# Moving the norm steps of the first batch to the wide tables in a two-layer graph attention kernel

## The chip, the cores and the metric

The kernel runs on one core of a Trainium2 chip. The metric is the device time of one execution in microseconds (us); lower is better. The core has a matrix engine (PE, with its weight loads shown apart as PEld), a vector engine (DVE), a scalar engine (ACT), GpSimd (POOL) and a queue that only issues transfers (SP). Each works through its own instructions in the order in which the program puts them there.

## The reference, cut to what matters

```
x = layernorm(x + L0(x, adj))          # x: (8, 2048, 256) f32, adj: (2048, 2048) int32
x = layernorm(x + L1(x, adj))

L0: q, k, v = x @ W.T + b              # 4 heads of 64
    s = clip(q k / 8, -10, 10); s = -10 where adj == 0
    softmax of s within each of 8 chunks of 256 keys; ctx = sum over chunks of attn @ v
    out = layernorm(ctx @ Wo.T + bo + x) * gamma + beta
L1: Wh = h @ W; e = leaky_relu(s_src + s_dst); softmax over the neighbours; elu(alpha @ Wh)
```

The result of the first line is called x1 below. Layer 1 needs x1 times W and times the two attention vectors (264 columns in all), with x1 turned so that its 256 features lie along the partitions.

## The kernel before, in words

The batches are taken one after the other. The attention of layer 0 of one batch is cut into 64 slots. Slot s stands for a query group q of 512 rows (q = s // 16, four groups), one of two head pairs and one of 8 key chunks; i = s % 16 is the place of the slot in its query group. In batch b the slots of layer 0 carry, interleaved, the layer 1 work of batch b-1 (lower.step, L799). Batch 0 has no layer 1 beside it. There the slots carry the mask steps instead (masks.step, L210), until they run out.

The order on every engine is written out by hand in the slot loop, L922 to L990. One slot does this, in this order:

- SP: the stores of the mask step before (send, L194), the mask piece of slot s+3 (load_slab, L361), and further loads named below.
- DVE: the reciprocal rd of slot s-1 (L427), then clip and mask of the scores of slot s+1, two instructions of 128x1024 that write pr (L388). They need the scores ps on PE (L377) and the slab.
- DVE: the norm steps that a table puts "beside" (L966).
- PE: product(s, 0) (L412), which needs the exponentials of slot s; then ACT: the copy raw (L419) and the two exponentials of slot s+1 (L400).
- The mask step (L976), where batch 0 still has one: SP loads a piece of adj (L216), PE turns the piece before it (L238), DVE writes clip (L240), ACT writes edge (L242), DVE writes ab (L228). The stores of clip and edge (L248, L251) go out at the head of the next slot, on SP. The tiles clip and edge have two buffers each, so that the clip of slot s waits until the clip of slot s-2 has been stored.
- PE: product(s, 1), ACT: its copy raw.
- The steps that tables put "behind" (L981 to L988): first those of the group before the current one (after), then the sending of a finished context, then those of the current group (behind).

From q = 1 on, an object Between (L501) carries query group q-1 through the rest of layer 0, between the slots of query group q. Its steps, with their instructions:

- Between(...) itself loads x into xg (512 KB, SP, L262).
- bias and shift: one DVE addition of 128x1024 each (L512, L516).
- output: 4 matmuls for two blocks of 128 rows (L527), into psM.
- add: DVE, from psM, two blocks (L538). stats: DVE, two blocks (L477, L480); the second call also makes rs and off (L485 to L488, DVE and POOL).
- a.apply: four ACT instructions (L492). scale, again: one DVE instruction each (L544, L547).
- finish: four ACT instructions, then ACT issues the store of x1 to x1D (L552).
- load: eight SP transfers of 64 KB that read x1D back in squares of 32x32 (L271, through load_squares). turn: one DVE transpose within squares (L283), which makes x1T.
- values of one block: matmuls of x1T with w1 (L571) into psM, and two ACT copies (L578, L582).

The context of a head pair goes out through ctxD (ACT) and comes back over SP (load_context, L447), and turn_context (L452, one DVE transpose of 128x512) writes it into qT. It stands at i = 3, and at i = 8+3 = 11, or at i = 8+6 = 14 where the flag wide is set (L961).

Which table is used is decided at i = 0 of each query group:

```
wide = b > 0 and 0 < q < NCH - 1
...
if not b:
    beside, behind, after = BESIDE_0, BEHIND_0, AFTER_0
```

So batch 0 uses the compact tables, with load at i = 12, turn and the first values at i = 15, and the other three values in the first three slots of the next query group. Batches 1 to 7 use the wide tables for q = 1 and 2. After slot 63 a list of pieces (order, L1022) finishes the batch; in batch 0 it begins with values 1, 2 and 3 of group 2.

Of the kernel before, what the change touches and what calls it, by code (L numbers as in the profile page):

```python
# [22 lines left out]
def adj_resnorm_kernel(  # L23
# [23 lines left out]
    NCH = N // CH  # L47
# [146 lines left out]
    def send():  # L194
        while outgoing:
            outgoing.pop(0)()
# [201 lines left out]
    def exps(s, u):  # L398
        pr = probs[s][u]
        nc.scalar.activation(pr, pr, AF.Exp, scale=0.125)  # L400
# [100 lines left out]
    class Between:  # L501
# [83 lines left out]

    AHEAD = {12: lambda o: o.load()}
    BESIDE = {  # L590
        1: [lambda o: o.bias()],
        4: [lambda o: o.add((0, 1))],
        5: [lambda o: o.add((2, 3)), lambda o: o.a.stats((0, 1))],
        6: [lambda o: o.a.stats((2, 3)), lambda o: o.shift()],
        8: [lambda o: o.scale()],
        9: [lambda o: o.again(), lambda o: o.b2.stats((0, 1))],
        10: [lambda o: o.b2.stats((2, 3))],
        14: [lambda o: o.turn()],
    }
    BEHIND = {  # L600
        3: lambda o: o.output((0, 1)),
        4: lambda o: o.output((2, 3)),
        7: lambda o: o.a.apply(o.y),
        11: lambda o: o.finish(),
        14: lambda o: o.values((0,)),
        15: lambda o: o.values((1,)),
    }

    WIDE_BESIDE = {
        1: [lambda o: o.bias()],  # L610
        4: [lambda o: o.add((0, 1))],
        5: [lambda o: o.add((2, 3))],
        6: [lambda o: o.a.stats((0, 1))],
        7: [lambda o: o.a.stats((2, 3))],
        8: [lambda o: o.shift()],
        10: [lambda o: o.scale()],
        11: [lambda o: o.again()],
# [3 lines left out]
    WIDE_BEHIND = {  # L621
        3: lambda o: o.output((0, 1)),
        4: lambda o: o.output((2, 3)),
        8: lambda o: o.a.apply(o.y),
        14: lambda o: o.finish(),
    }
    LATER_AHEAD = {0: lambda o: o.load()}
    LATER_BESIDE = {2: lambda o: o.turn()}
    LATER_BEHIND = {i: lambda o, i=i: o.values((i - 5,)) for i in range(5, 9)}

    BESIDE_0 = {i: steps for i, steps in BESIDE.items() if i != 14} | {15: BESIDE[14]}
    BEHIND_0 = {i: step for i, step in BEHIND.items() if i != 14} | {15: BEHIND[14]}
    AFTER_0 = {i: lambda o, i=i: o.values((i + 1,)) for i in range(3)}
    AFTER = {0: lambda o: o.values((2,)), 1: lambda o: o.values((3,))}

    def factors(b, sd, waug):

# [268 lines left out]
    for b in range(B):  # L906
        waug = blocks.tile([P, NT, H, D1], F32, tag="waug", name="waug")
        sd = small.tile([P, 2 * H, NT], F32, tag="sd", name="sd", bufs=1)
        if b == 0:
            for s in range(3):  # L910
                load_slab(s)
            scores(0)
            for u in range(KT):
                exps(0, u)
        if lower:
            for _ in range(STEP):
                lower.make()
        closing = Closing(b - 2, CLOSING) if b > 1 else None
        if closing:
            closing.do(-1)  # L920
        group = None
        for s in range(SLOTS):  # L922
            q, hp, c = where[s]
            i = s % QS
            send()
            if s + 3 < SLOTS:
                load_slab(s + 3)
            if i == 0:
                before = group
                group = Between(b, q - 1, sd, waug) if q else None  # L930
                wide = b > 0 and 0 < q < NCH - 1
                ahead = {} if wide else AHEAD
                later_beside = {}
                if not b:
                    beside, behind, after = BESIDE_0, BEHIND_0, AFTER_0
                else:
                    beside, behind = (WIDE_BESIDE, WIDE_BEHIND) if wide else (BESIDE, BEHIND)
                    after = {}
                    if q > 1:
                        later_beside, after = LATER_BESIDE, LATER_BEHIND  # L940
            if before and later_beside and i in LATER_AHEAD:
                LATER_AHEAD[i](before)
            if i == 1 and q:
                load_context(b, q - 1, 1)
            if i == QS // 2 + 1:
                load_context(b, q, 0)
            if group and i in ahead:
                ahead[i](group)
            if s == SLOTS - 3 and b + 1 < B:
                turns = [project(b + 1, g) for g in range(NCH)]  # L950
                turns[0].pop(0)()
            if s:
                normalize(s - 1)
            if s + 1 < SLOTS:
                scores(s + 1)

            if s == SLOTS - 1 and b + 1 < B:
                turns[0].pop(0)()
            if i == 3 and q:
                turn_context(q - 1, 1)  # L960
            if i == QS // 2 + (6 if wide else 3):  # L961
                turn_context(q, 0)
            if before and i in later_beside:
                later_beside[i](before)
            if group:
                for step in beside.get(i, ()):  # L966
                    step(group)
            elif closing:
                closing.do(s, behind=False)
            product(s, 0, not lower)  # L970
            if s + 1 < SLOTS:
                for u in range(KT):
                    exps(s + 1, u)
            if lower:
                if b + 1 < B or s < SLOTS - LATE:
                    lower.step()  # L976
            elif masks.left():
                masks.step()
            product(s, 1, not lower)

            if before and i in after:  # L981
                after[i](before)
            if i == 0 and q:
                send_context(b, q - 1, 1)
            if i == QS // 2:
                send_context(b, q, 0)
            if group and i in behind:
                behind[i](group)  # L988
            elif closing and not q:
                closing.do(s, beside=False)  # L990
        normalize(SLOTS - 1)

        send()
        before = group
        gd, fs = factors(b, sd, waug)
        group = None
        every = tuple(range(QT))

        def begin():
            nonlocal group  # L1000
            group = Between(b, NCH - 1, sd, waug)

        def ctx():
            context(NCH - 1, 1)

        steps = [
            lambda: group.bias(),
            lambda: group.output(every),
            lambda: group.add(every),
            lambda: (group.shift(), group.a.stats(every)),  # L1010
            lambda: group.a.apply(group.y),
            lambda: (group.scale(), group.again(), group.b2.stats(every)),
            lambda: group.finish(),
            lambda: group.turn_all(),
            lambda: group.values((0, 1)),
            lambda: group.values((2, 3)),
        ]
        if b + 1 < B:
            (k0, v0, q0), (l1, t1, k1, v1, q1), (l2, t2, k2, v2, q2), (l3, t3, k3, v3, q3) = turns
            rest = [lambda: lower.rest(1)] if lower else []  # L1020
            first = [] if b else [lambda: before.values((1,))]
            order = [begin, *rest, l1, *rest, *first, lambda: before.values((2, 3))]  # L1022
            order += [*rest, ctx, *rest, k0]
            order += [steps[0], t1, steps[1], v0, steps[2], steps[3], l2, k1, steps[4], q0]
            order += [steps[5], v1, t2, l3, steps[6], q1, steps[7], k2, steps[8], steps[9], t3, v2]
            order += [lambda: [load_slab(s) for s in range(3)], fs[0], q2, fs[1], k3, fs[2], v3]
            order += [lambda: scores(0), q3, lambda: [exps(0, u) for u in range(KT)]]
        else:

            step = lower.step  # L1030
            order = [begin, lambda: before.values((2, 3)), steps[0], step, ctx, step, steps[1], step]
            order += [steps[2], step, steps[3], step, steps[4], step, steps[5], step, steps[6], step]
            order += [steps[7], step, steps[8], step, steps[9], step, fs[0], step, fs[1], step, fs[2]]
            order += [step, lambda: lower.rest(4)]
            assert sum(p is step for p in order) == LATE
        for piece in order:
            send()
            piece()
        send()
        lower = Layer1(b, gd, waug)  # L1040
# [56 lines left out]
```

## Time and profile before

| | |
|---|---|
| median of 4 runs | 3794.96 us (3793.72 to 3796.33) |
| the profiled execution's own time | 3796.46 us |
| its span in the profile | 3794.7 us |
| mean granted PE clock | 0.992 |
| PE busy | 3680.2 us (97%) |
| DVE busy | 3196.1 us (84%) |
| ACT busy | 1946.9 us (51%) |
| POOL busy | 1388.1 us (37%) |
| slots of batch 0 with i = 0, by the reciprocal of the slot | slot 16 at 140.23, slot 32 at 229.89, slot 48 at 309.08 |
| last reciprocal of the slot loop of batch 0 (slot 63) | 381.29 us |
| first layer 1 instruction (L734) | 447.9 us |

In timelines, a line gives the start in us from the start of the span, the duration in us, the engine, the line of the kernel, the operation, the tile written and the tile read, the count, and in brackets how long the engine had been idle before and what ended that. A small q behind an engine's name is its queue of transfers. In tables by stretch, each engine has its busy time and its count of instructions; then come the granted PE clock (1.00 is full), the share of time in which the DMA engines were busy, and GB/s. In lists of waits, the three numbers are the total in us, how often, and the longest.

### The profile page before, as it was taken

To read this page: it belongs to the slowest core of one execution; us is meant where nothing else is said; L and a number is where in the kernel's file an instruction comes from. 1 tells how busy PE (TensorE), PEld (TensorE's weight loads), DVE (VectorE), ACT (ScalarE), POOL (GpSimd) and SP (SyncE) were. 2 spreads that over 40 slices of the span, in tenths; PEclk is the share of its full clock that TensorE was granted. 3 is DMA by queue.
4 is the path that set the end of the run, shared out by engine and by line. 5 is a ranking of instruction groups with operands and counts; after the bars stand their busy time and mean duration, and the time that the engine had idled before them with its cause. 6 is when DMAs were issued, how large, how long until landed. Compare 5 with 4: busy or idle time off the path is not lost. (4 is left out here: it accounts for less than half of the span.)

```text
span 3794.7 us, 160217 instructions
## 1 busy us (share of the span) xinstructions
PE 3680.2 (97%) x72100; PEld 2747.4 (72%) x72100; DVE 3196.1 (84%) x4810; ACT 1946.9 (51%) x3601; POOL 1388.1 (37%) x1202
## 2 busy tenths in 40 slices
PE   9999999999999999999999999999999999999787
PEld 5656677776777777776777767777677777776676
DVE  5876499986999789995999959998699968998798
ACT  4666345555555555554555545554555555555221
POOL 1445234433343343433444324433344434434310
PEclk9999999999999999999999999999999999999899
DMA  6652333333343433433434434433333334333354
GB/s 162 150 115 65 79 102 101 97 88 113 106 105 96 94 115 102 103 97 88 134 88 104 102 98 127 105 100 82 113 107 104 101 88 121 98 103 81 97 151 120
DMA packets 756545, 398.50 MB, mean 105 GB/s; under 512 B 425744, under 2 KB 721040, under 8 KB 755856
## 3 DMA queue, kind: packets, MB, share of 16 engines
q1 hardware_dynamic: 705856, 354.54, 36.1%
q10 hardware_dynamic: 50000, 33.70, 2.8%
q8 instruction: 564, 9.24, 1.0%
q14 instruction: 125, 1.02, 0.1%
HBM read 331.22 MB, written 56.89 MB: 102 GB/s over the span
## 5 line engine op out<-in xcount | busy, mean ns | idle before, releaser
L388 DVE SCALAR_TENSOR_TENSOR pr<-ps,slab 128x1024 f32<-128x1024 f32 x1024 | 1191.5, 1204 | 198.9 <-PE ps L377 194.2
L734 DVE SCALAR_TENSOR_TENSOR e<-srow,gd,et 128x640 f32<-128x640 f32 (+1 forms) x1536 | 1344.6, 931 | 11.4 <-PE pa L754 6.2
L412 PEld LDWEIGHTS pc<-vaug,pr 128*64 128x64 f32 x32768 | 1039.7, 138 | 411.6 <-issue 302.8
L412 PE MATMUL pc<-vaug,pr 128*64 128x65 f32 x32768 | 1156.4, 224 | 18.0 <-ACT raw L419 10.5
L754 PE MATMUL pa<-waug,e 128*64 128x65 f32 x32768 | 1081.0, 224 | 39.4 <-DVE e L734 38.0
L400 ACT ACTIVATE pr<-pr 128x1024 f32<-128x1024 f32 x1024 | 1045.3, 1056 | 74.3 <-DVE pr L388 63.1
L754 PEld LDWEIGHTS pa<-waug,e 128*64 128x64 f32 x32768 | 1020.2, 139 | 64.6 <-DVE e L734 37.7
L377 PE MATMUL ps<-qT,kT 64*128 64x512 f32 x4096 | 1025.4, 617 | 3.3 <-DVE pr L388 2.4
L419 ACT COPY raw<-pc 128x260 f32<-128x260 f32 x1024 | 384.7, 376 | 1232.8 <-PE pc L412 1206.5
L434 POOL TENSOR_TENSOR part<-raw,rd 128x512 f32<-128x512 f32 x448 | 467.9, 1044 | 1426.5 <-DVE rd L427 1412.1
L436 POOL TENSOR_TENSOR acc<-acc,part 128x512 f32<-128x512 f32 x448 | 574.9, 1283 | 35.2
L377 PEld LDWEIGHTS ps<-qT,kT 64*128 64x128 f32 x4096 | 349.8, 186 | 328.5 <-issue 223.3
L427 DVE RECIPROCAL rd<-raw 128x8 f32<-128x8 f32 x512 | 100.6, 197 | 102.7 <-ACT raw L419 101.0
L434 POOL TENSOR_TENSOR acc<-raw,rd 128x512 f32<-128x512 f32 x64 | 66.8, 1043 | 318.6 <-DVE rd L427 317.8
L782 ACT ACTIVATE hh<-pa,dn 128x64 f32<-128x64 f32 x512 | 114.8, 321 | 101.0 <-DVE dn L778 101.0
L571 PE MATMUL pw<-w_sb,x1T 128*128 128x264 f32 x512 | 140.6, 411 | 9.9 <-DVE x1T L283 9.4
L487 POOL TENSOR_TENSOR rs_c<-rs_c,nhalf 128x4 f32<-128x4 f32 x32 | 55.6, 1737 | 229.4 <-DVE off_c L486 229.4
L321 PE MATMUL pp<-xT,wk_sb 128*128 128x512 f32 x256 | 119.8, 612 | 7.9 <-ACT qT L329 6.6
L527 PE MATMUL po<-wo_sb,qT 128*128 128x256 f32 x512 | 125.0, 389 | 1.1 <-DVE qT L454 0.8
L321 PE MATMUL pp<-xT,wq_sb 128*128 128x512 f32 x256 | 116.2, 596 | 0.0
L337 PE MATMUL pv<-wv_sb,xT 128*128 128x256 f32 x512 | 115.9, 379 | 0.0
L571 PEld LDWEIGHTS pw<-w_sb,x1T 128*128 128x128 f32 x512 | 92.6, 194 | 31.5 <-DVE x1T L283 10.0
(93 smaller groups left out, 1858.1 us busy)
## 6 DMA issues: line engine op xcount, KB each, us to landing
et<-edgeD SPq DMA_DIRECT2D x256, 320.0 KB, 3.1
slab<-clipD SPq DMA_DIRECT2D x512, 128.0 KB, 3.3
et<-edgeD SPq DMA_DIRECT2D x128, 384.0 KB, 3.4
srow<-rowD SPq DMA_DIRECT2D x64, 320.0 KB, 4.3
xg<-in_x_dram SPq DMA_DIRECT2D x32, 512.0 KB, 5.4
x1D<-y ACTq DMA_DIRECT2D x32, 512.0 KB, 4.2
x1g<-x1D SPq DMA_DIRECT2D x32, 512.0 KB, 5.5
out_dram<-o SPq DMA_DIRECT2D x32, 512.0 KB, 3.9
```

The source lines that it names most:

```text
L321: nc.tensor.matmul(pps[c], lhsT=w[:, kc, c * P : (c + 1) * P], rhs=st["xT"][:, kc, :], start=(kc == 0), stop=(kc == KC - 1),)
L377: nc.tensor.matmul(ps[:, k, :], lhsT=kT[rows, hp, t * P : (t + 1) * P], rhs=qT[rows, hp, cols], start=True, stop=True,)
L388: nc.vector.scalar_tensor_tensor(pr, pss[u], -CLIP, slab[:, u, :].unsqueeze(1).to_broadcast([P, 2, CH]), op0=ALU.max, op1=ALU.min,)
L400: nc.scalar.activation(pr, pr, AF.Exp, scale=0.125)
L412: nc.tensor.matmul(pc[z * D : (z + 1) * D, i, :], lhsT=probs[s][u][:, k, i * P + z * D : i * P + (z + 1) * D], rhs=vaug[:, KT * c + u, 2 * ...
L419: nc.scalar.copy(raws[s][:, k], pc)
L434: nc.gpsimd.tensor_mul(part, raw[:, :, :, :D], rd.to_broadcast([P, 2, QT, D]))
L436: nc.gpsimd.tensor_add(accv, accv, part)
L527: nc.tensor.matmul(po[:, k, :], lhsT=qT[:, c, t * P : (t + 1) * P], rhs=wo_sb[:, c, :], start=(c == 0), stop=(c == KC - 1),)
L571: nc.tensor.matmul(pw[:, k, : F + 2 * H], lhsT=self.x1T[:, c, u * P : (u + 1) * P], rhs=w1_sb[:, c, :], start=(c == 0), stop=(c == KC - 1),)
L734: nc.vector.scalar_tensor_tensor(e[:, :w], self.rows[n][:, :w], self.gd[:, h, j : j + 1], self.edge[k // JG][:, j % JG, :w], op0=ALU.max, ...
L754: nc.tensor.matmul(self.pa[z * D : (z + 1) * D, i * D1 : (i + 1) * D1], lhsT=e[:, i * P + z * D : i * P + (z + 1) * D], rhs=self.waug[:, j ...
```

## The change

The flag wide no longer depends on the batch, and the special tables AFTER_0 and AFTER are gone. In batch 0, groups 0 and 1 (in q = 1 and q = 2) now take the wide tables, and their load, turn and values move into the next query group by the LATER tables, as in the other batches. Group 2 (in q = 3) keeps BESIDE_0 and BEHIND_0. The other batches and the pieces after slot 63 are as before. The program has the same number of rows on PE and on SP in both versions.

| step | i before (batch 0, groups 0 and 1) | i after |
|---|---|---|
| load of x | 0 | 0 |
| bias | 1 | 1 |
| output, two halves (behind) | 3, 4 | 3, 4 |
| add, two halves | 4, 5 | 4, 5 |
| stats of the first norm | 5, 6 | 6, 7 |
| shift | 6 | 8 |
| apply (behind) | 7 | 8 |
| scale | 8 | 10 |
| again | 9 | 11 |
| stats of the second norm | 9, 10 | 12, 13 |
| finish (behind) | 11 | 14 |
| turn_context of the first head pair | 11 | 14 |
| load of x1 in squares (head of the slot) | 12 | 0 of the next q, after the load of x |
| turn | 15 | 2 of the next q |
| values of four blocks (behind) | 15, and 0, 1, 2 of the next q | 5, 6, 7, 8 of the next q |

```
-    AFTER_0 = {i: lambda o, i=i: o.values((i + 1,)) for i in range(3)}
-    AFTER = {0: lambda o: o.values((2,)), 1: lambda o: o.values((3,))}
...
-                wide = b > 0 and 0 < q < NCH - 1
+                wide = 0 < q < NCH - 1
                 ahead = {} if wide else AHEAD
-                later_beside = {}
-                if not b:
-                    beside, behind, after = BESIDE_0, BEHIND_0, AFTER_0
+                if wide:
+                    beside, behind = WIDE_BESIDE, WIDE_BEHIND
                 else:
-                    beside, behind = (WIDE_BESIDE, WIDE_BEHIND) if wide else (BESIDE, BEHIND)
-                    after = {}
-                    if q > 1:
-                        later_beside, after = LATER_BESIDE, LATER_BEHIND
+                    beside, behind = (BESIDE, BEHIND) if b else (BESIDE_0, BEHIND_0)
+                later_beside, after = (LATER_BESIDE, LATER_BEHIND) if q > 1 else ({}, {})
             if before and later_beside and i in LATER_AHEAD:
                 LATER_AHEAD[i](before)
```

## The prediction, as put on record before the run

> **What bounds the kernel now.** I first read the page: PE is busy 97% of 3794.7 us, but the change touches only slots 16 to 63 of batch 0, 140 to 385 us. So I took that stretch apart, by waits, by DVE and PE timelines, and by SP's own queue. A slot is told by its reciprocal rd (L427); I call "rd(s)" the one in slot s.
>
> The DVE timeline of slots 29 to 32 (rd at 217.05, 224.47, 229.89):
>
> ```profile
> 217.05 0.20 DVE L427 RECIPROCAL rd<-raw 128x8 f32<-128x8 f32 x1 [0.92 <-ACT raw L419]
> 217.17 2.34 DVE L388 SCALAR_TENSOR_TENSOR pr<-ps,slab 128x1024 f32<-128x1024 f32 x2
> 222.54 0.82 DVE L240 TENSOR_SCALAR clip<-pm 128x640 int8<-128x640 bf16 x1 [3.03 <-DMA clipD<-clip]
> 223.28 0.48 DVE L228 TENSOR_SCALAR ab<-araw 128x640 bf16<-128x640 int32 x1
> 224.47 0.20 DVE L427 RECIPROCAL rd<-raw 128x8 f32<-128x8 f32 x1 [0.71 <-ACT raw L419]
> 224.59 2.34 DVE L388 SCALAR_TENSOR_TENSOR pr<-ps,slab 128x1024 f32<-128x1024 f32 x2
> 226.85 1.23 DVE L283 STREAM_TRANSPOSE x1T<-x1t 128x1024 f32<-128x1024 f32 x1
> 229.89 0.20 DVE L427 RECIPROCAL rd<-raw 128x8 f32<-128x8 f32 x1 [0.71 <-ACT raw L419]
> 232.32 1.22 DVE L388 SCALAR_TENSOR_TENSOR pr<-ps,slab 128x1024 f32<-128x1024 f32 x1 [2.22 <-DMA slab<-clipD]
> ```
>
> Two stalls stand here: clip waits 3.03 for a store, and pr waits 2.22 in slot 32. SP's queue shows where the first comes from:
>
> ```profile
> 206.91 0.53 SPq L364 DMA_DIRECT2D slab<-clipD  x1
> 211.69 5.00 SPq L271 DMA_DIRECT2D x1t<-x1D  x8
> 216.73 0.49 SPq L216 DMA_DIRECT2D araw<-in_adj_dram  x1
> 217.31 0.38 SPq L248 DMA_DIRECT2D clipD<-clip  x1
> ```
>
> The load of x1 at i = 12 comes straight behind the finish at i = 11. SP stands from 207.4 to 211.7 for the store of x1 and then needs 5.0 for eight transfers. The store of slot 28's clip, queued behind, goes out at 217.31 only, and clip of slot 30 waits for it. The second stall is PE's, in spite of its label: that slab went out at 221.77, and the longest landing of a slab here is 4.8, so it lay there by 226.6.
>
> ```profile
> 228.13 2.13 PE L571 MATMUL pw<-w_sb,x1T 128*128 128x264 f32 x4 [2.47 <-DVE x1T L283]
> 230.19 3.58 PE L377 MATMUL ps<-qT,kT 64*128 64x512 f32 x8
> ...
> 308.83 1.16 PE L571 MATMUL pw<-w_sb,x1T 128*128 128x264 f32 x4 [1.93 <-DVE x1T L283]
> ...
> 314.94 1.99 PE L377 MATMUL ps<-qT,kT 64*128 64x512 f32 x8
> ```
>
> Values of block 0 stand in the slot of their own turn; PE waits 2.47 for it (group 0) and 1.93 (group 1). Group 0's matmuls then take 2.13 and 3.58 instead of 1.16 and 1.99, since the clock is halved:
>
> ```profile
> 224.00:228.00 4.00, 1.52 (x37) 1.28 (x36) 3.53 (x4) 2.75 (x5) 2.32 (x2) 0.83 0.95 225
> 228.00:232.00 4.00, 3.87 (x8) 2.02 (x10) 1.39 (x4) 1.44 (x5) 1.68 (x2) 0.50 0.45 81
> ```
>
> **Two kinds of slot.** With a mask step (until slot 36) a plain slot takes 4.51 (4.61 with masks of 768 columns). Its chain is rd, pr, pr, extra DVE work x, clip, edge on ACT, raw, next rd. The bias slot (x = 1.14 net) takes 5.43, the scale slot (1.37) 5.66, the one with stats and shift (2.28) 6.57: 4.29 + x. So x costs itself, less 0.22 once per slot. Without masks a slot takes 3.93 from scores to scores, which is PE's own 1.99 + 2.09 less overlap; DVE has about 1.46 idle there and ordinary extras are nearly hidden, but one block of values costs 1.09 in full (slots 49 and 50: 5.02).
>
> **What the Trainium skill says.** "TensorE: Matmul & The Clock Gate", part 1 on the HAM clock gate, says that PE falls to half its clock after an idle window of about 3.4 us and recovers after as long a busy one. The trace agrees: 0.50 in the stretch after gaps of 2.37 and 2.47 us, though neither alone is that long. "DMA: Bandwidth & Descriptors", Specifications, puts line rate at transfers of 512 B or more. x1 is read back in runs of 32 floats, 128 B; the DMA share was 0.96 and 1.00 in the two stretches of 4 us from 216, with a store landing 5.2 us after issue. The same first page, under the array's architectural detail, has ACT and DVE as strict FIFO: clip's wait above held up everything behind it on DVE, which agrees.
>
> **The change, part by part.** No work is added or dropped; I sum slot lengths, before against after.
>
> *Slots 16 to 31 (group 0).* Before they sum to 229.89 - 140.23 = 89.66. Slots 16 to 20 stay (25.58). Slot 21 loses its stats (0.87): 6.82 to 5.95. Slots 22, 23, 24 hold stats (0.87), stats with rs and off (1.14), shift (1.14 and a little for wider masks): 5.16, 5.43, 5.47. Slot 25 follows apply and has nothing on DVE to cover it. The finish of before delayed the exponentials of slot 28 by 1.27 and cost 1.09; apply has no store to issue and delays them by some 0.9, so I put 0.7: 5.3. Before, the scale slot (5.66 = 4.29 + 1.37) covered this. Slots 26 to 29: scale 5.91, again 5.73, stats 5.4, stats 5.43. Slot 30: turn_context (0.62), 4.91 instead of 7.42, as nothing blocks SP any more. Slot 31 follows finish: 5.6, against 5.42 with turn. New sum 85.87: **-3.8**.
>
> *Slots 32 to 36.* Before: from rd(32) = 229.89 to the scores at 261.24 in slot 37, 31.35. After: plain 4.51, bias 5.43, turn (1.15) 5.44, turn_context 4.91, then 6.13 as from rd(20) = 159.66 to the scores at 165.79: 26.42. **-4.9**. In it are the PE wait, the slow clock and three blocks of values that leave; the turn that arrives costs 0.93.
>
> SP at slot 32: x1 load now stands behind slab and xg. Finish runs from rd(31) on, its store is issued 1.9 later and landed by 4.9 (208.74 to 211.69 before), while slot 31 lasts 5.6: no wait for the store. Eight issues end at rd(32) + 6 and land 2.4 later, at + 8.4; turn stands at rd(34) + 2.4 = + 12.3. Margin 4. The stores of slot 32's clip go out at + 7 and, at 5.2, land by + 12.2; clip in slot 34 is due at + 13.4. Margin about 1. ctx loads behind them are due in slot 35 only; xg has 5.9 before bias against a landing of 4.3.
>
> *Slots 37 to 47.* Before, scores to scores, 261.24 to 309.92: 48.68. After: four slots with values at 5.02 (stats and shift fit into the DVE idle), slots 41 to 46 at 4.15, 4.2, 4.1, 3.95, 3.95, 3.93 (apply hides behind values' PE time; scale and again cost 0.2 to 0.3 as now), slot 47 behind finish 4.95 (before, slot 44: 5.0). Sum 49.3, against 48.68 that held one block of values and a wait of 1.93: **+0.6**. The cover that four values of before partly had (bias slot with values 5.65, without 5.43: only 0.2) is lost here.
>
> *Slots 48 to 56.* Three values and the tail of the x1T wait leave the first slots, four arrive at slots 53 to 56. Before, nine intervals from 309.92 to 353.06, 43.14; after 3.93, 3.95, 3.95 (turn hidden), 5.85, 6.17, 5.03, 5.02, 5.07, and 5.2 (4.20 before, and 1.09 less a little cover): 44.2. **+1.1**. Turn at slot 50 is due 15.2 after rd(47), and x1 landed 12.7 after the corresponding rd(44): margin 2.5.
>
> Sum: -3.8 - 4.9 + 0.6 + 1.1 = **-7.0**. The profiled execution, 3796.46 (span 3794.7 and 1.8 around it), becomes 3789.5; it stood 1.5 above the median, so the median 3794.96 becomes **3788.0**. This is 0.18%, just inside the 0.2% that a measurement of this kernel can tell from no change.
>
> Unknowns, both ends: uncovered apply 0 to 1.1 (taken 0.7); excess of slots 41 to 46 0 to 1.3 (0.7); SP margins 0 to 3. Nothing excludes a gain beyond the sum, as any hole in PE now closed may also have cost clock.
>
> **The rivals.** (1) *Better cover.* If apply and the second norm vanish wholly in the spread order and finish is half hidden: 0.7 + 0.7 + 0.8 more, -9.2, 3785.8. For it: DVE idle of 1.46 per slot without masks. Against: such slots before still ran 4.2 to 4.3. (2) *The stall moves.* DMA engines at share 1.00, and stores of masks queued behind xg and x1; clip of slot 34 waits as clip of slot 30 did, 3 us: -4.0, 3791.0. Against: the wait for the x1 store, 4.3 of the 9.3 that SP was shut, is gone. (3) *Slower: turn waits and holds DVE.* Turn in slots 34 and 50 now stands before clip and the next pr, so a late x1t stops all engines. If SP is shut as long as its longest wait for x1 (9.8) on both, the waits over the margins are 5.8 + 7.3 = 13.1, and two falls to half clock at 2.6 each make 18.3: +11.3, 3806.3. It decides for "slower than before" once the two waits pass 7.0 together. Against: the store has a slot of time now. (4) *Nothing*: the stalls only covered other waits, 0, 3795.
>
> **How the numbers follow.** Forecast 0.62, with its own range 3786 to 3790, of which 0.24 lies below 3787.4; rival 1 0.16, rival 2 0.14, rival 3 0.04, rival 4 0.04. Faster by over 0.2%: 0.24 + 0.16 = 0.40; slower 0.05 (rival 3, and 0.01 of rival 4); within 0.2% the rest, 0.55. The range reaches to rivals 1 and 2: 3784.5 to 3792.5.
>
> **What would show it.** No clip wait over 1 us and no clock of 0.50 between slots 28 and 34; x1T followed by its values three slots later with no PE wait on L283; rd(32) near 226.1; scores of slot 57 near 346; values in slots 37 to 40 at 5.0 each. Wrong if clip, turn or bias wait for DMA in slots 33, 34 or 50, or if slots 25 and 41 to 47 run over 5.5.

## The result, and the profile after

| | before | changed |
|---|---|---|
| median, first comparison | 3795.5 us (51 runs) | 3788.62 us (33 runs) |
| ratio, 95% interval | | 0.9982 (0.9977 to 0.9987) |
| median, second comparison | 3798.54 us (19 runs) | 3790.15 us (15 runs) |
| ratio, 95% interval | | 0.9978 (0.9970 to 0.9986) |
| profiled execution: span | 3794.7 us | 3787.1 us |
| rd of slot 16 to rd of slot 63 | 241.06 us | 233.18 us |

The change gains 6.9 us in the first comparison and 8.4 in the second; 7.0 was forecast. In the two profiles it is 7.6 of span, and the slots 16 to 63 alone, the stretch that was changed, are 7.88 shorter.

DVE's timeline of the changed kernel, slots 30 to 32 and slot 34. The stalls of before are gone:

```profile
217.72 0.70 DVE L454 STREAM_TRANSPOSE qT<-ctx 128x512 f32<-128x512 f32 x1
218.34 0.78 DVE L240 TENSOR_SCALAR clip<-pm 128x640 int8<-128x640 bf16 x1
220.23 0.20 DVE L427 RECIPROCAL rd<-raw 128x8 f32<-128x8 f32 x1 [0.71 <-ACT raw L419]
...
225.83 0.20 DVE L427 RECIPROCAL rd<-raw 128x8 f32<-128x8 f32 x1 [2.01 <-ACT raw L419]
225.95 2.34 DVE L388 SCALAR_TENSOR_TENSOR pr<-ps,slab 128x1024 f32<-128x1024 f32 x2
...
238.14 1.23 DVE L283 STREAM_TRANSPOSE x1T<-x1t 128x1024 f32<-128x1024 f32 x1
239.30 0.79 DVE L240 TENSOR_SCALAR clip<-pm 128x640 int8<-128x640 bf16 x1
```

Neither clip has a wait in brackets any more, and the turn stands in slot 34 without a wait for x1t. The 2.01 ahead of rd(32) is the price of the finish, which moved from slot 27 to slot 30.

SP's queue in slot 32 (the line of x1t holds the first six of its eight transfers), then the first and the fourth values of group 0 on PE:

```profile
225.90 1.53 SPq L364 DMA_DIRECT2D slab<-clipD  x1
227.53 0.39 SPq L262 DMA_DIRECT2D xg<-in_x_dram  x1
228.00 4.27 SPq L271 DMA_DIRECT2D x1t<-x1D  x6
...
234.11 0.38 SPq L248 DMA_DIRECT2D clipD<-clip  x1
```

```profile
256.44 1.13 PE L571 MATMUL pw<-w_sb,x1T 128*128 128x264 f32 x4 [0.23 <-PE pc L412]
257.50 1.99 PE L377 MATMUL ps<-qT,kT 64*128 64x512 f32 x8
...
271.47 1.16 PE L571 MATMUL pw<-w_sb,x1T 128*128 128x264 f32 x4
```

SP goes straight from xg to x1t: the store of x1 went out on ACT at 222.13, a whole slot earlier, so SP no longer stands still for it, only issues. PE does not wait for x1T, and its matmuls run at full speed. The table by stretch has clock 1.00 where it had 0.50:

```profile
224.00:228.00 4.00, 3.39 (x73) 2.67 (x73) 2.17 (x3) 2.92 (x5) 1.74 (x2) 1.00 0.52 124
228.00:232.00 4.00, 4.00 (x79) 2.66 (x75) 3.08 (x6) 2.84 (x6) 1.62 (x2) 1.00 0.84 222
```

### The profile page after: what moved, and what is told of

Its sections match the earlier page's. It is cut to its first block, busy times and chain, and to the rows that moved or that the text cites. A ratio compares the mean times of both kernels' runs of the same rounds, so it can differ in the third digit from the quotient of the medians.

```text
span 3787.1 us, 160213 instructions
## 1 busy us (share of the span) xinstructions
PE 3677.4 (97%) x72100; PEld 2747.7 (73%) x72100; DVE 3196.2 (84%) x4810; ACT 1945.9 (51%) x3601; POOL 1385.6 (37%) x1202
## 5 line engine op out<-in xcount | busy, mean ns | idle before, releaser
L751 PE MATMUL pa<-waug,e 128*64 128x65 f32 x32768 | 1080.9, 224 | 40.0 <-DVE e L731 38.4
L751 PEld LDWEIGHTS pa<-waug,e 128*64 128x64 f32 x32768 | 1020.8, 139 | 64.6 <-DVE e L731 38.1
```

Of the source, the lines that this page charges most:

```text
L751: nc.tensor.matmul(self.pa[z * D : (z + 1) * D, i * D1 : (i + 1) * D1], lhsT=e[:, i * P + z * D : i * P + (z + 1) * D], rhs=self.waug[:, j ...
```

## The experiments

My theory was that the gain is the end of three stalls: SP shut by a load right behind its store (clip of slot 30), the fall of PE's clock (slot 32), and PE's wait for x1T (slot 48). The rival was the change's own description: the norm steps spread over more slots balance DVE. The runs came in three groups, each with its own runs of before; ratios and gains in us are to those. A ratio is not the quotient of the two medians (for the first run that would be 0.9979), so the two can tell gains that differ by some 2 us. The sums are of slot lengths, rd to rd, in one profile of each run; in the row of the changed kernel they are from the profile shown above.

| run | median us | ratio to before (95% interval) | slots 16-31 | 32-47 | 48-62 |
|---|---|---|---|---|---|
| before | 3795.87 to 3798.54 | | 89.66 | 79.19 | 72.21 |
| changed | 3790.15 | 0.9978 (0.9970, 0.9986) | 86.52 | 77.22 | 69.44 |
| late load, compact order | 3788.7 | 0.9973 (0.9964, 0.9983) | 85.84 | 77.15 | 69.44 |
| spread order, early load | 3805.9 | 1.0020 (1.0012, 1.0028) | 86.52 | 86.22 | 74.90 |
| load at 13 | 3793.22 | 0.9989 (0.9982, 0.9995) | 86.75 | 76.57 | 71.85 |
| values one slot later | 3793.68 | 0.9991 (0.9985, 0.9998) | 88.65 | 76.15 | 71.34 |
| both single moves | 3787.77 | 0.9976 (0.9967, 0.9986) | 86.76 | 74.65 | 69.50 |
| changed, x earlier | 3784.38 | 0.9966 (0.9954, 0.9979) | 86.54 | 77.75 | 69.44 |
| late load, compact order, x earlier | 3780.82 | 0.9958 (0.9946, 0.9970) | 85.85 | 77.16 | 69.45 |
| the same, last values moved too | 3783.61 | 0.9964 (0.9950, 0.9977) | 85.84 | 77.16 | 69.45 |
| both single moves, x earlier | 3782.32 | 0.9959 (0.9946, 0.9971) | 86.77 | 74.65 | 69.51 |

A profile is one execution. Three profiles of the changed order give 77.22, 77.37 and 77.75 for slots 32 to 47, and where only these slots changed, the gain in their sums differs from the gain in the medians by up to 2.5 us (load at 13: 5.9 against 3.6). The slots tell where time went; how much the change is worth, only the medians tell.

**Late load alone.** Against the changed kernel:

```
-                wide = 0 < q < NCH - 1
-                ahead = {} if wide else AHEAD
-                if wide:
+                wide = b > 0 and 0 < q < NCH - 1
+                late = 0 < q < NCH - 1
+                ahead = {} if late else AHEAD
+                if late and not b:
+                    beside, behind = EARLY_BESIDE, EARLY_BEHIND
+                elif wide:
...
+    EARLY_BESIDE = {i: steps for i, steps in BESIDE.items() if i != 14}
+    EARLY_BEHIND = {i: step for i, step in BEHIND.items() if i < 14}
```

> Groups 0 and 1 of batch 0 keep the compact norm steps and the finish at i = 11; only load, turn and values stand where the change puts them. Theory of the stalls (gain = no closed SP queue, no x1T wait, no half clock): all three stalls are gone, so 6 to 8 us below before, rd(16) to rd(32) near 86, no clip wait over 1 us, clock 1.00 throughout slots 28 to 36. Rival (the gain is the spread of the norm steps over more slots): at most 2 us below before.

Measured: 0.9973, 8.1 us under before, no less than the changed kernel. Slots 16 to 31 take 85.84 against 86.52. No clip waits in slots 30 to 34, and the clock is 1.00 from 204 to 252 us. So the spread order gave nothing; in slots with mask steps it costs some 0.7 us. Most of that is probably apply, which has nothing on DVE beside it any more: slot 25 takes 5.10 where a slot without norm steps takes 4.61.

**Spread order alone.** Against the changed kernel, the load of x1 stands right behind its finish again, now at i = 14 and 15:

```
-                ahead = {} if wide else AHEAD
+                ahead = ({} if b else {15: AHEAD[12]}) if wide else AHEAD
...
+                if not b and q > 1:
+                    after = SOON_BEHIND
-            if before and later_beside and i in LATER_AHEAD:
+            if b and before and later_beside and i in LATER_AHEAD:
...
+    SOON_BEHIND = {i: lambda o, k=k: o.values((k,)) for k, i in enumerate((2, 5, 6, 7))}
```

> Groups 0 and 1 of batch 0 take the spread norm steps, but the load of x1 stands at the head of i = 15, right behind the finish at i = 14, and values of block 0 in the slot of the turn (i = 2 of the next query group), the others at 5, 6, 7. Theory of the stalls: SP is shut some 9 us again from slot 31, clip of slot 33 waits 2 to 3 us, PE waits for x1T in slots 34 and 50 (1.5 to 2.5 each): 0 to 2 us below before. Rival (the spread brings the gain): 5 to 7 us below before.

Measured: 9.1 us slower than before. Both expectations missed, 0 to 2 and 5 to 7 us below. The wait that I expected on clip came on another transfer, the load of x into xg, which stood behind the load of x1 on SP. SP, DVE and PE in slots 31 to 33:

```profile
227.42 5.07 SPq L271 DMA_DIRECT2D x1t<-x1D  x8
...
234.78 0.47 SPq L262 DMA_DIRECT2D xg<-in_x_dram  x1
...
241.15 1.22 DVE L512 TENSOR_TENSOR xg<-xg,bo_sb 128x1024 f32<-128x1024 f32 x1 [6.05 <-DMA xg<-in_x_dram]
...
236.22 1.15 PE L412 MATMUL pc<-vaug,pr 128*64 128x65 f32 x32
243.89 0.69 PE L238 MATMUL pm<-identb,ab 128*128 128x128 bf16 x5 [6.52 <-ACT edge L242]
```

```profile
236.00:240.00 4.00, 1.37 (x34) 1.01 (x32) 0.00 (x0) 0.20 (x1) 0.00 (x0) 0.91 0.99 264
240.00:244.00 4.00, 0.11 (x2) 0.21 (x3) 2.36 (x3) 0.85 (x2) 0.00 (x0) 0.50 0.70 135
244.00:248.00 4.00, 2.63 (x38) 2.24 (x36) 3.78 (x5) 2.51 (x4) 2.32 (x2) 0.50 0.74 163
```

The last fence is the table by stretch. bias waits 6.05, clip and edge stand behind it, PE idles 6.52 and comes back at half clock: slot 33 takes 11.57 us and slot 35 still 8.18. It is the mechanism of rival 3, a late load that holds DVE, at another step. In the changed kernel the load of x1 comes after xg on SP, and bias in slot 33 does not wait. As this collision is new, the run shows that the spread order alone does not bring the gain; what the order is worth, the run before it shows.

**The load one slot later, nothing else.** Against before:

```
                 ahead = {} if wide else AHEAD
+                if not b and 0 < q < NCH - 1:
+                    ahead = {13: AHEAD[12]}
```

> The kernel before with one step moved: the load of x1 of groups 0 and 1 of batch 0 one slot later, i = 13. Theory of the stalls: SP no longer waits for the store of x1, only issues 5 us, so clip of slot 30 waits under 1 us; slot 30 falls from 7.42 to about 4.6 to 5, slot 32 stays over 7: 2.5 to 4 us below before. Rival (the spread brings the gain): within 1 us of before.

Measured: 3.6 us under before by the medians (ratio 0.9989). Slot 30 fell from 7.42 to 4.51, as expected. Slot 32 did not stay over 7: it fell from 8.31 to 5.74. PE in this run, and its clock:

```profile
223.94 1.16 PE L571 MATMUL pw<-w_sb,x1T 128*128 128x264 f32 x4 [1.98 <-DVE x1T L283]
225.03 1.99 PE L377 MATMUL ps<-qT,kT 64*128 64x512 f32 x8
```

```profile
224.00:228.00 4.00, 4.00 (x44) 2.32 (x44) 2.99 (x5) 1.32 (x4) 1.87 (x2) 1.00 0.58 118
```

SP issues the load at 212.21, right behind a slab, without a stand. PE still waits 1.98 for x1T, but at full clock. The 2.57 that slot 32 lost are the clock: at half clock the values and the scores behind them took 0.97 and 1.59 longer. The other 1.23 over a plain slot (5.74 against 4.51) stay with the wait. That the clock had fallen because the gap of 2.37 that clip's stall left on PE stood close before that wait is likely, but it is argued from one profile each, and the wait itself was 0.49 shorter here.

**Values one slot later, nothing else.** Against before:

```
-    AFTER_0 = {i: lambda o, i=i: o.values((i + 1,)) for i in range(3)}
+    AFTER_0 = {i: lambda o, i=i: o.values((i,)) for i in range(4)}
...
+                    if q < NCH - 1:
+                        behind = {k: step for k, step in BEHIND_0.items() if k != 15}
```

> The kernel before with the values of groups 0 and 1 of batch 0 one slot later (i = 0 to 3 of the next query group), so that none stands in the slot of its turn. Theory of the stalls: no PE wait for x1T of groups 0 and 1, no clock of 0.50 before slot 60, slot 32 at about 5.5 instead of 8.31 and slot 48 at about 5.0 instead of 6.66, while the clip wait of slot 30 stays: 3 to 5 us below before. Rival (the spread brings the gain): within 1 us of before.

Measured: 3.1 us under before by the medians. Slot 32 fell to 4.50, slot 48 to 3.91, and clip of slot 30 still waited, though only 1.52. Up to that point this is the program of before, where it waited 3.03: the stall itself changes from one execution to the next. About 2.2 each came back in slots 36 and 52 (8.63 for 6.39, 8.04 for 5.86): the fourth block now shared a slot with output, which waits for psM.

```profile
247.58 0.20 ACT L582 COPY sd<-pw 128x8 f32<-128x8 f32 x1
247.84 1.99 PE L527 MATMUL po<-wo_sb,qT 128*128 128x256 f32 x8 [1.08 <-ACT sd L582]
```

**Both single moves.** Load at 13, and the values at 0, 1, 2 and 5, clear of output:

```
-    AFTER_0 = {i: lambda o, i=i: o.values((i + 1,)) for i in range(3)}
+    AFTER_0 = {i: lambda o, k=k: o.values((k,)) for k, i in enumerate((0, 1, 2, 5))}
...
+                if not b and 0 < q < NCH - 1:
+                    ahead = {13: AHEAD[12]}
...
+                    if q < NCH - 1:
+                        behind = {k: step for k, step in BEHIND_0.items() if k != 15}
```

> The kernel before with the two single moves together: load of groups 0 and 1 at i = 13, values at i = 0, 1, 2 and 5 of the next query group. No spread order and no late load or turn. Theory of the stalls: all the gain of the change is there, 6 to 9 us below before. Rival (late load and turn themselves matter): 4 us below before or less.

Measured: 8.1 us under before, 0.9976. The whole gain of the change is there with the load one slot later and the four blocks of values at 0, 1, 2 and 5 instead of 15, 0, 1 and 2, and no spread order.

**The same fault at the end of batch 0.** There group 2 still loads x1 right behind its finish, and x for the next batch queues behind that. Against the changed kernel:

```
-            if group and i in ahead:
-                ahead[i](group)
-            if s == SLOTS - 3 and b + 1 < B:
+            if s == (SLOTS - 3 if b else SLOTS - 5) and b + 1 < B:
                 turns = [project(b + 1, g) for g in range(NCH)]
                 turns[0].pop(0)()
+            if group and i in ahead:
+                ahead[i](group)
```

> The changed kernel, and at the end of batch 0 the load of x for the next batch stands two slots earlier (slot 59 instead of 61), ahead of the load of x1 of group 2, which comes behind its finish as it did for the other groups. Theory of the stalls (a load right behind finish shuts SP and lets PE fall to half clock): the DVE wait of 3.5 us for xp in slot 63 goes, and with it most of the PE wait of 4.5 us for x1T: 2 to 5 us below the changed kernel, 9 to 12 below before. Rival (that wait lies beside other work, the end of the batch is bound by x of the next group and by PE): same as the changed kernel within 1 us.

Measured: 3784.38, 11.5 under before (the changed kernel was 6.9 and 8.4 under, beside other runs of before). In the changed kernel DVE waited for xp and PE for x1T, and the clock fell. SP, DVE and PE, then the table by stretch:

```profile
364.49 4.80 SPq L271 DMA_DIRECT2D x1t<-x1D  x8
369.33 4.92 SPq L271 DMA_DIRECT2D xp<-in_x_dram  x8
...
376.23 1.25 DVE L283 STREAM_TRANSPOSE xT<-xp 128x1024 f32<-128x1024 f32 x1 [3.54 <-DMA xp<-in_x_dram]
378.66 2.13 PE L571 MATMUL pw<-w_sb,x1T 128*128 128x264 f32 x4 [4.51 <-DVE x1T L283]
```

```profile
380.00:384.00 4.00, 3.46 (x8) 2.21 (x8) 1.23 (x1) 0.89 (x4) 1.21 (x1) 0.50 1.16 203
```

With x two slots earlier the same places of DVE and PE, and the table, read:

```profile
375.51 1.25 DVE L283 STREAM_TRANSPOSE xT<-xp 128x1024 f32<-128x1024 f32 x1
377.94 1.16 PE L571 MATMUL pw<-w_sb,x1T 128*128 128x264 f32 x4 [1.06 <-DVE x1T L283]
```

```profile
380.00:384.00 4.00, 4.00 (x19) 3.01 (x18) 1.22 (x1) 1.60 (x5) 0.51 (x1) 1.00 0.91 136
```

Slot 63, which is not in the sums above, fell from 6.04 to 2.59.

**Combinations.** The compact order with the late load and the early x is the edit of the first run and that of the run before together:

> Compact norm steps with the late load, turn and values, and the early load of x of the run before. If the two act apart: the sum of both, 10 to 14 us below before, and not slower than the changed kernel with the early load. If the spread order is worth something: 1 us or more slower than that one.

Measured: 3780.82, 15.1 under before, the fastest median of all. Beside the spread order with the early x, in the same group, it is 3.6 faster, but the two intervals overlap, and the slots account for 1.3 of it (86.54 + 77.75 against 85.85 + 77.16).

Taking the last values out of slot 63 as well:

```
+    LAST_BEHIND = {i: step for i, step in BEHIND.items() if i < 14}
...
-                    beside, behind = (BESIDE, BEHIND) if b else (BESIDE_0, BEHIND_0)
+                    beside, behind = (BESIDE, BEHIND) if b else (BESIDE_0, LAST_BEHIND if q == NCH - 1 else BEHIND_0)
...
-            first = [] if b else [lambda: before.values((1,))]
+            first = [] if b else [lambda: before.values((0,)), lambda: before.values((1,))]
```

> As the run with compact norm steps and the early load of x, and values of block 0 of group 2 leave the slot of their turn for the pieces after slot 63. Theory of the stalls: PE no longer waits for x1T in slot 63, so as fast or up to 2 us faster than without this move, 11 to 15 us below before. Rival: the wait is only moved to the next piece, no difference.

Measured: 3783.61, no gain to be seen. PE's wait for x1T stays at 1.1, as the rival had it: the values became the first piece after the slots that PE meets, and nothing was put ahead of them.

Both single moves with the early x:

> The kernel before with the two single moves (load at i = 13, values at 0, 1, 2 and 5 of the next query group) and the early load of x for the next batch. Here three of the four blocks of values of group 0 stand in slots that have a mask step, where PE has idle time; in the changed kernel all four stand in slots bound by PE. If that cover is worth the 1.5 us of the forecast: 1 to 3 us below the compact order with the late load and the early load of x, that is 13 to 17 below before. If not: the same as that one.

Measured: 0.9959 against 0.9958 for the compact order with the late load. Its slots 32 to 47 are 2.5 shorter and its slots 16 to 31 0.9 longer; the times do not tell the two apart. So the lost cover of values shows in slots but is not shown in the time. The changed kernel ran beside it:

> The changed kernel itself, once more, beside the runs of this call: 6 to 8 us below before, by the forecast and by its first result.

Measured: 8.4 under before, a little over what was expected.

## Why the prediction was right

Its sum, term by term, against the profile after:

| stretch | forecast | measured |
|---|---|---|
| slots 16 to 31 | -3.8 | -3.14 |
| slots 32 to 36 (rd(32) to the scores of slot 37) | -4.9 | -4.97 |
| slots 37 to 47, scores to scores | +0.6 | -0.80 |
| slots 48 to 56, scores to scores | +1.1 | +2.75 |
| slot 57 to rd(63) | 0 | -1.72 |
| together | -7.0 | -7.88 |

The mechanism was right: the stalls that it named are gone, and the first two stretches carry the gain. That the total came so close is in part luck. The terms that were forecast come to -6.16; the other -1.72 lie in slots 57 to 63, where nothing was forecast, and the errors of -1.40 and +1.65 in the two stretches before that nearly cancel. The rule of two kinds of slot held in the slots with masks: slots 22, 23, 26, 28 and 29 were forecast at 5.16, 5.43, 5.91, 5.4 and 5.43 and took 5.16, 5.44, 5.90, 5.41 and 5.43. Slot 30 took 4.89 (4.91 forecast), slot 32 took 4.51 (4.51). One slot was clearly off. Slot 21 took 6.39, not 5.95: stats left DVE, but the scores came 0.95 late there and ACT's chain behind them, exponentials, edge and raw, still set the end; rd(22) waited 1.15 for raw. Slots 24 and 27 were 0.1 and 0.3 longer than forecast.

In the slots without masks the total was near the forecast but its place was not. Forecast, slots 37 to 56: +1.7; measured: +1.95. PE kept its 3.93 to 3.94 without excess in slots 41 to 46, where I had put 0.7, and the delay behind finish showed only after the scores of slot 48; in slot 51 output waited 0.71 for turn_context as well. That the excess of before in slots 57 to 59 (4.46, 4.49 and 4.21 from scores to scores instead of 3.93) would also go, -1.72 with what followed, I had not seen: scores of slot 57 were put near 346 (they came at 345.98, but rd(16) already stood 0.92 earlier than before, ahead of all that was changed) and the rest left alone. Of my unknowns, uncovered apply came out at 0.5 (slot 25: 5.10 against 4.61), near the 0.7 taken.

The stalls were read rightly, and the single moves show it: each alone gives a part, both together give all. But the split of slot 32 was not in the prediction. It named PE's wait for x1T and the clock together; the load at 13 shows that of the 3.80 over a plain slot the clock was 2.57 and the wait of some 2 us with its block of values 1.23. A block of values without the wait costs nothing there (slot 33 took 5.43 with one, in the run with the values one slot later, and 5.43 without in the changed kernel), so a slot with masks has some PE time to spare. In slot 48, without masks, the wait cost 1.64 of its 1.93 (6.66 against 5.02 for the next slots with values). What the prediction gave to slots 16 to 31 rests on clip's stall of 3.03, which was half as long in another execution of the same instructions.

Rivals. Better cover: half came, in slots 41 to 46 and 57 to 59, and finish was not hidden. It isn't due to the spread order, as the late load with the compact order has the same sums there (77.15 and 69.44). The stall on clip did not move, and in the profile after the margin of 1 us on its store held. It was thin: in the run with x earlier, the same program up to slot 59, clip of slot 34 waited for its store, and slots 33 and 34 took 5.66 and 5.73 instead of 5.43 and 5.42:

```profile
242.00 0.82 DVE L240 TENSOR_SCALAR clip<-pm 128x640 int8<-128x640 bf16 x1 [0.19 <-DMA clipD<-clip]
```

The slower case did not occur in the change, but the run with the spread order and the early load shows its mechanism, at xg instead of x1t. The Trainium skill's statement that ACT and DVE are strict FIFO ("TensorE: Matmul & The Clock Gate", the array's architectural detail) is what makes it dear, and the trace agrees: clip, which stands behind bias on DVE, began at 242.30 only, after bias had waited 6.05 us.

## What to carry to other kernels

Before moving compute steps, look in the timeline of the issuing queue for a load that waits for a store issued just ahead of it: here all transfers behind it on that queue waited with it, those that other engines needed first among them. Moving one such load a slot later, or behind the transfers that others need first, gave here what rearranging a dozen vector steps seemed to give. To know which part of a change works, make each part alone, and compare slot by slot, as the total hides parts that cancel.

## What the runs showed that I had not expected

The length of a gap on PE does not tell whether its clock falls. Gaps of 2.37 and 2.47 us with 1.5 us of work between them brought 0.50; gaps of 1.98 and 1.06 did not; gaps of 4.51 (with two of 0.7 to 0.8 ahead of it) and 6.52 did. It looks as if nearby gaps add up, but that does not fit all the traces either. In the run with the spread order PE had worked without a gap from 232 us until 237.37 (236.22 + 1.15), and the mean of 0.91 in the stretch to 240 puts the fall, by estimate, at 239.3, after 1.9 us of idle (the ends of matmuls are modelled in the trace). And in the last batch, whose program is the same in both kernels (L754 became L751), 20 matmuls stand behind a gap of 1.64, before at full clock and after at half clock:

```profile
3583.42 0.80 PE L754 MATMUL pa<-waug,e 128*64 128x65 f32 x20 [1.64 <-DVE e L734]
...
3576.05 1.35 PE L751 MATMUL pa<-waug,e 128*64 128x65 f32 x20 [1.64 <-DVE e L731]
```

The Trainium skill ("TensorE: Matmul & The Clock Gate", part 1) gives an idle window of about 3.4 us. As a length of idle that PE must reach first, these traces do not bear it out, nor does the pair of gaps in the prediction, which was put there as agreeing; what decides stays open here. The price is plain: in the profile before, a stall of 3 us was billed twice, 2.9 in its own slot and, with the clock, 2.6 in the next but one.
